# Gated cross-attention block: values by seven block products, the output projection in one place

## Chip, core and metric

The kernel runs on one NeuronCore of a Trainium2 chip. The metric is the device time of one execution in microseconds; the median of three runs is given. Profiles are one execution each.

The engines are called as in the profile: PE is TensorE (PEld its weight loads), DVE is VectorE, ACT is ScalarE, POOL is GpSimd, SP is SyncE, which only issues DMAs here.

## What is computed

There are 8 batches of a 512 x 2048 matrix x (features by sequence), a context c of the same shape, and a mask. All is float32.

```python
xn = layernorm(x)                              # over the sequence axis
q, k = Wq @ patch(xn) + bq, Wk @ patch(xn) + bk   # patches of 128 columns, 256 rows
v = Wv @ patch(c) + bv                         # 256 rows
attn = softmax(mask(q_h.T @ k_h / sqrt(32)))   # 8 heads of 32 rows, 128 x 128 in each patch
o = gelu(v_h @ attn.T)
x1 = x + tanh(g_xattn) * mask * (Wo @ o + bo)
flat = layernorm(x1)                           # over the sequence again; rows are the 512 features
s = softmax(flat @ router.T + rb)              # 64 experts
w = the 8 largest of s, the others zero
out = x1 + tanh(g_ffn) * (flat * sum(w) + w @ expert_bias)
```

## The kernel before

The sequence of each batch is cut into chunks of 512 columns, four per batch, 32 in all. A chunk has two halves of 256 columns (two patches each). One pass of the main loop, a *slot* `g`, handles the scores and the exponentials of one half: `ch = g // 2`, an even slot for the first half and an odd one for the second. Work of other chunks is mixed into the slot by hand. There is no automatic scheduler: each engine runs its instructions in the order of the program text, and tiles bring the waits.

In slot `g` of chunk `ch` the program does, in this order of the text:

1. `scores(g)`: four PSUM banks `sc0` to `sc3` (pool `ps_sc`, one buffer each) take the mask product (L433) and the score products (L442).
2. `weigh(g-2)` and `weighed(g-2)`: attention times values into a bank `tr`, copied to `o` by ACT (L515).
3. `maxima`, `exps` (DVE L454, ACT L463), `divide` (a reciprocal on DVE, L471, and a 128 x 1024 product on POOL, L472), and `turn`/`turned` (PE transposes of the slot before, L486, and ACT copies, L492).
4. `queries_and_keys(ch+1, h)`: half of the rows of q and k of the next chunk, by seven block products in place of eight. Its sums s1, s5, u2, u3 are on DVE, u4 on POOL (L387), and the second half of k (L395) adds u4. `sums_of_x` prepares the sums of xn on POOL (L300 to L305).
5. `values(ch+1, h)`: v of one half of the next chunk, 8 products of 128 x 256 (L410) into a bank `mm`, evicted by one DVE addition (`values_out`, L419).
6. `attend`: the output projection of the chunk before, 4 row blocks `m` of 512 columns (L534), each evicted by DVE (L540) into `t` and added to x on POOL (L543). Blocks 0 and 1 stand at the end of the odd slot; blocks 2 and 3 follow the scores of the next even slot.
7. `turn_x`, `logits`, `statistics2` (L553), and, per batch in turn, `aggregate` (L246 to L254), `gather`, `choose`, `select`, `turn_weights`: the router for the batch that is complete. `fin` is `g % 8` for that batch: 2 aggregates, 3 gathers, 4 selects.
8. `scale_x` (POOL, L678) and `mix` (PE L691, DVE L702, then the store): the expert mix of a batch that is twelve slots behind.

Reads of x for the statistics of the next batch (`stats_x`, L263) are on DVE near the slot's end. The last two slots, 62 and 63, are written out after the loop.

The pools that matter: `ps_mm` and `ps_tr` have two banks each, `ps_sc` four; `cx` (a half of c) has two buffers, `o` two, `mk` four. All large loads and stores are issued on SP.

Of the kernel before, what the change touches and what calls it, by code (L numbers as in the profile page):

```python
# [35 lines left out]
def flamingo_gated_kernel(  # L36
# [74 lines left out]

    def load_cx(ch, h, queue=nc.sync):
        t = work.tile([P, NM, HW], F32, tag="cx", name=f"cx_{ch}_{h}")
        s0 = (ch % NCH) * CW + h * HW
        queue.dma_start(t, rows_of(c, ch // NCH, slice(s0, s0 + HW)))
        cxs[ch, h] = t

    def load_mask(ch):
        t = work.tile([P, CW], F32, tag="mk", name=f"mk_{ch}", bufs=4)
        nc.sync.dma_start(t, masks[ch // NCH, :, columns(ch)].to_broadcast([P, CW]))  # L120
        mks[ch] = t
# [33 lines left out]
    load_first_x(0)  # L155
    load_cx(0, 1)
    nc.sync.dma_start(wq_sb, wqT.rearrange("(m p) e -> p m e", p=P))
    nc.scalar.dma_start(wk_sb, wkT.rearrange("(m p) e -> p m e", p=P))
    load_first_x(1)

    def load_rest():
        load_cx(1, 0)
        load_first_x(2)
        load_first_x(3)
        load_mask(0)
        nc.sync.dma_start(bv_sb, bv.partition_broadcast(P))
        with nc.allow_non_contiguous_dma(reason="short bias vectors onto partitions"):
            nc.sync.dma_start(bq_sb, bq.rearrange("(t p) -> p t", p=P))
            nc.sync.dma_start(bk_sb, bk.rearrange("(t p) -> p t", p=P))
            nc.sync.dma_start(bo_sb, bo.rearrange("(t p) -> p t", p=P))  # L170
        nc.sync.dma_start(gates[:, 0:1], g_xattn.partition_broadcast(P))
        nc.sync.dma_start(gates[:, 1:2], g_ffn.partition_broadcast(P))
        nc.sync.dma_start(rb_sb, rb.partition_broadcast(P))
        load_mask(1)
# [11 lines left out]
    for i in range(2):  # L186
        nc.vector.tensor_copy(
            ident2[i * E : (i + 1) * E, :], ident[i * E : (i + 1) * E, i * E : (i + 1) * E]
        )
    ones = const.tile([P, P], F32, name="ones")  # L190
    nc.vector.memset(ones, 1.0 / S)

# [228 lines left out]


    pairs = {}

# [86 lines left out]
    def weighed(g):  # L511
        ch, hf = g // NH, g % NH
        if hf == 0:
            os_[ch] = work.tile([P, NE, CW], F32, tag="o", name=f"o_{ch}")
        nc.scalar.copy(  # L515
# [78 lines left out]

    def gather(b, ms=range(NM)):

        t = experts[b]
        if 0 in ms:
            t["pg"] = ps_tr.tile([P, NM, E], F32, tag="tr", name=f"pg_{b}")
            t["lg"] = small.tile([P, NM, E], F32, tag="lg", name=f"lg_{b}", bufs=1)  # L600
        for m in ms:
            nc.tensor.matmul(  # L602
                t["pg"][:, m, :], lgT[b][:, m * P : (m + 1) * P], ident2, start=True, stop=True
            )

    def gathered(b):
        t = experts[b]
        nc.scalar.copy(t["lg"], t["pg"])
        t["pg"] = t["lg"]

# [44 lines left out]
    def turn_weights(b):  # L655
        t = experts[b]
        rest = t.pop("rest")
        wT = small.tile([P, NM // 2, P], F32, tag="wT", name=f"wT_{b}", bufs=1)
        pw = product([P, NM // 2, P], f"pw_{b}", None if late else 1)
        for mp in range(NM // 2):  # L660
# [115 lines left out]
    def centre_router():  # L776

        pr = ps_tr.tile([P, E], F32, tag="tr", name="pr")
        nc.tensor.matmul(pr, ones, rwsum, start=True, stop=True)
        nc.vector.tensor_tensor(  # L780
            rw_sb, rw_sb, pr[:, None, :].to_broadcast([P, NK, E]), ALU.subtract
        )
# [6 lines left out]
    for g in range(NG - NH):  # L789
# [14 lines left out]
        pch = ch - 1 if not even and ch >= 1 else None  # L804

        vals = [] if (nxt, h) == (1, 0) or nxt == last else [(nxt, h)]
        b4 = ch // NCH - 1
# [12 lines left out]
        if even:  # L820
            if nxt > 1:
                load_cx(nxt, 1)
            if nxt < last and nxt + 1 >= NCH:
                load_xn(nxt + 1)
        elif nxt < last:
            load_cx(nxt + 1, 0)
        if even and NCH <= ch - 1:
            load_xr(ch - 1)

# [17 lines left out]
        if even:  # L847
            if xch is not None:
                for m in (2, 3):
                    attend(xch, m)  # L850
                del os_[xch], mks[xch]
            exps(g, 1)
            exps(g, 2)
            if g > 0:
                mask(nxt)
            turn_(0)
            turn_(1)
# [4 lines left out]
            if g > 0:  # L862
                divide(g, 0)
            if g == 0:
                load_mask(2)
        else:
# [17 lines left out]
        def between(i):  # L884
            if even:
                if g == 0 and i == 0:
                    divide(g, 0)
                    mask(nxt)
                turn_x_(i)
            elif i == 0:  # L890
                if g == 1:
                    divide(g, 0)
                turn_(1)
                if fin == 3:
                    gather(b4)
                    gathered(b4)
                if pch is not None:
                    gelu(pch)
            else:
                turn_(2)  # L900
                if pch is not None and nxt < last:
                    load_mask(nxt + 1)

# [32 lines left out]
        if even:  # L936
            turn_x_(2)
            for c_, h_ in vals:
                values(c_, h_, 0, 0)
                turn_(2)  # L940
                values(c_, h_, 1)
            if not vals:
                turn_(2)
            if nxt < last and (nxt + 1) % NCH:
                norm(nxt + 1, (0, 1))
            for c_, h_ in vals:
                values_out(c_, h_)
            if fin == 4:
                stats()
            if fin == 4:  # L950
                turn_weights(b4)
            turn_x_(3)
            turn_(3)
            if nxt < last and (nxt + 1) % NCH:
                norm(nxt + 1, (2, 3))
            if fin == 4:
                for k in steps:
                    scale_x(mb, k)
        else:
# [3 lines left out]
            if fin == 3:  # L963
                choose_exps(b4)
            for c_, h_ in vals:
                values(c_, h_, 0, 0)
                values(c_, h_, 1)
                values_out(c_, h_)
            if pch is not None:
                for m in (0, 1):  # L970
                    attend(pch, m, r=m + 1)
            if nxt < last:
                sums_of_x(nxt + 1, 1)
                sums_of_x(nxt + 1, 2)
        if g == 1:
            nc.scalar.activation(wo_sb, wo_sb, AF.Copy, scale=tgates[:, 0:1])
        if g == 2:
            router_sums()
        if g == 3:
            centre_router()  # L980
# [21 lines left out]
    maxima(h0, (2, 3))  # L1002
    exps(h0, 0)
    exps(h0, 1)
    for m in (2, 3):
        attend(z - 2, m, tag=t_raw)
    divide(h0, 0)
    turn_(h0 - 1, 0, 1)
    exps(h0, 2)
    values(z, 0, 0)  # L1010
    turn_(h0 - 1, 2)
    exps(h0, 3)
    values(z, 0, 1)
    values_out(z, 0)
    turn_(h0 - 1, 3)
    divide(h0, 1)

# [6 lines left out]
    exps(g, 0)  # L1024
    mix(b - 1, 2)
    turn_(h0, 1)
    exps(g, 1)
    divide(g, 0)
    values(z, 1, 0)
    turn_x(z - 2, 0, nc.vector)  # L1030
    exps(g, 2)
    values(z, 1, 1)
    values_out(z, 1)
    exps(g, 3)
    divide(g, 1)
    turn_(h0, 2)
    turn_x(z - 2, 1, nc.vector)
    turn_(h0, 3)
    turn_x(z - 2, 2, nc.vector)
    gelu(z - 1)  # L1040
    mix(b - 1, 3)
    load_xr(z)
    turn_x(z - 2, 3, nc.vector)
    weigh(h0)
# [112 lines left out]
```

## Time and profile before

| what | us |
|---|---|
| median of 3 runs | 1337.61 |
| lowest to highest | 1336.63 to 1337.97 |
| the profiled execution, device time | 1337.72 |
| its span, first to last instruction | 1335.9 |
| PE busy | 1306.5 |
| DVE busy | 887.2 |
| ACT busy | 836.0 |
| POOL busy | 793.1 |
| an even slot in the middle (655.98 to 675.90) | 19.92 |

The mean granted TensorE clock is 0.995 of full speed. An idle time in the profile's rows stands in brackets, with what ended it. Busy times overlap: they say how much an engine has to do, not which one the others wait for. The order in which one engine's rows stand and the start times tell that.

### The profile page before, as it was taken

To read this page: it belongs to the slowest core of one execution; us is meant where nothing else is said; L and a number is where in the kernel's file an instruction comes from. 1 tells how busy PE (TensorE), PEld (TensorE's weight loads), DVE (VectorE), ACT (ScalarE), POOL (GpSimd) and SP (SyncE) were. 2 spreads that over 40 slices of the span, in tenths; PEclk is the share of its full clock that TensorE was granted. 3 is DMA by queue.
4 is the path that set the end of the run, shared out by engine and by line. 5 is a ranking of instruction groups with operands and counts; after the bars stand their busy time and mean duration, and the time that the engine had idled before them with its cause. 6 is when DMAs were issued, how large, how long until landed. Compare 5 with 4: busy or idle time off the path is not lost.

```text
span 1335.9 us, 26509 instructions
## 1 busy us (share of the span) xinstructions
PE 1306.5 (98%) x9802; PEld 953.6 (71%) x9802; DVE 887.2 (66%) x1815; ACT 836.0 (63%) x2843; POOL 793.1 (59%) x802
## 2 busy tenths in 40 slices
PE   7999999999999999999999999999999999999997
PEld 4677777777777777777777777777777777777653
DVE  5666666576766766677666676667676675666566
ACT  2567756666755666756667566667656767656653
POOL 3545556565566755667555667556566665566652
PEclk8999999999999999999999999999999999999999
DMA  9423332334443534443534443524544423332124
GB/s 290 117 73 124 98 103 99 131 105 133 150 163 115 166 102 136 150 146 131 166 100 138 151 148 130 166 89 135 165 146 132 156 65 120 135 112 87 64 80 173
DMA packets 109729, 173.32 MB, mean 130 GB/s; under 512 B 9248, under 2 KB 43680, under 8 KB 109472
## 3 DMA queue, kind: packets, MB, share of 16 engines
q1 hardware_dynamic: 107536, 168.75, 39.1%
q10 hardware_dynamic: 2064, 2.88, 0.6%
q8 instruction: 77, 1.26, 0.4%
q14 instruction: 52, 0.43, 0.1%
HBM read 138.06 MB, written 33.55 MB: 128 GB/s over the span
## 4 chain that ended last, share of the span: by engine, by line
PE 93%; DVE 3%; ACT 2%; DMA 1%; issue 0%; DVEq 0%; ACTq 0%
PE qk L373 27%; PE po L534 17%; PE pv L410 15%; PE pt L486 8%; PE pa L505 5%; PE pb L691 5%; PE pl L572 4%; PE sc L442 4%; PE px L558 4%; PE sc L433 2%; ACT at L463 1%; PE pf L339 1%; DMA cx<-in_ctx 1%; DVE st L553 1%; DVE st L263 1%; PE pg L602 1%
## 5 line engine op out<-in xcount | busy, mean ns | idle before, releaser
L472 POOL TENSOR_TENSOR at<-at,rsum 128x1024 f32<-128x1024 f32 x128 | 244.3, 1908 | 282.2 <-DVE rsum L471 259.6
L463 ACT ACTIVATE at<-sc,nmx 128x128 f32<-128x128 f32 x1024 | 364.9, 415 | 5.8 <-DVE nmx L454 5.8
L463 ACT ACTIVATION_READ_ACCUMULATOR at<-sc,nmx 128x1 f32 x1024 | 261.4, 255 | 0.0
L410 PE MATMUL pv<-wv_sb,cx 128*128 128x256 f32 x1024 | 242.7, 386 | 9.8 <-DMA cx<-in_ctx 9.6
L534 PE MATMUL po<-o,wo_sb 128*128 128x512 f32 x512 | 234.0, 599 | 0.0
L410 PEld LDWEIGHTS pv<-wv_sb,cx 128*128 128x128 f32 x1024 | 191.4, 194 | 33.8 <-DMA cx<-in_ctx 10.0
L543 POOL TENSOR_TENSOR xr<-t,xr 128x512 f32<-128x512 f32 x124 | 160.4, 1294 | 88.7 <-DVE t L540 88.2
L515 ACT COPY o<-pa 128x512 f32<-128x512 f32 x64 | 37.5, 585 | 258.2 <-PE pa L505 258.2
L492 ACT COPY atT<-pt 128x512 f32<-128x512 f32 x256 | 151.4, 622 | 56.2 <-PE pt L486 55.7
L454 DVE TENSOR_REDUCE nmx<-sc 128x4 f32<-128x512 f32 x256 | 158.7, 682 | 12.0 <-PE sc L442 12.0
L534 PEld LDWEIGHTS po<-o,wo_sb 128*128 128x128 f32 x512 | 94.2, 190 | 100.1 <-issue 92.8
L540 DVE SCALAR_TENSOR_TENSOR t<-po,bo_sb,mk 128x512 f32<-128x512 f32 x128 | 95.9, 750 | 100.6 <-PE po L534 99.9
L486 PEld LDWEIGHTS pt<-ident,at 128*128 128x128 f32 x1024 | 122.0, 141 | 56.9 <-issue 36.4
L486 PE MATMUL pt<-ident,at 128*128 128x128 f32 x1024 | 150.8, 275 | 1.3 <-ACT atT L492 1.1
L563 ACT COPY x1T<-px 128x512 f32<-128x512 f32 x120 | 70.3, 585 | 118.8 <-PE px L558 117.1
L373 PE MATMUL qk<-xt,wq_sb 128*128 128x256 f32 x496 | 128.2, 381 | 1.3 <-DVE u L381 1.3
L373 PE MATMUL qk<-xn,wk_sb 128*128 128x256 f32 x496 | 127.6, 380 | 0.0
L373 PE MATMUL qk<-xn,ws 128*128 128x256 f32 x496 | 127.3, 379 | 0.0
L373 PEld LDWEIGHTS qk<-xn,ws 128*128 128x128 f32 x496 | 94.2, 190 | 12.8
L702 DVE TENSOR_TENSOR xr<-pb,xr 128x512 f32<-128x512 f32 x124 | 79.2, 684 | 33.0 <-PE pb L691 33.0
L373 PEld LDWEIGHTS qk<-xn,wk_sb 128*128 128x128 f32 x496 | 89.3, 190 | 10.0 <-DVE lgT L588 0.3
L678 POOL TENSOR_SCALAR xr<-xr,xa,xd 128x512 f32<-128x512 f32 x120 | 94.4, 797 | 0.8
(119 smaller groups left out, 2008.4 us busy)
## 6 DMA issues: line engine op xcount, KB each, us to landing
cx<-in_ctx SPq DMA_DIRECT2D x63, 512.0 KB, 5.4
out_dram<-xr SPq DMA_DIRECT2D x60, 512.0 KB, 3.5
raw<-in_x SPq DMA_DIRECT2D x112, 256.0 KB, 3.5
xn<-in_x SPq DMA_DIRECT2D x28, 1024.0 KB, 7.5
xr<-in_x SPq DMA_DIRECT2D x28, 1024.0 KB, 7.8
mk<-in_mask_Bx1x_ff SPq DMA_DIRECT2D x32, 256.0 KB, 5.4
xr<-in_x SPq DMA_DIRECT2D x10, 256.0 KB, 5.9
out_dram<-xr SPq DMA_DIRECT2D x7, 256.0 KB, 2.3
```

What stands on the lines that cost most here:

```text
L373: nc.tensor.matmul(out_, w_[:, j, es], xb[:, j, :], start=(j == 0), stop=(j == NM // 2 - 1))
L410: nc.tensor.matmul(pv[:, i, :], cx[:, m, i * W : (i + 1) * W], wv_sb[:, m, :], start=(m == 0), stop=(m == NM - 1),)
L454: nc.vector.tensor_reduce(p["nmx"][:, r, :, :], p["sc"][r], AX.X, ALU.max, negate=True)
L463: nc.scalar.activation(p["at"][i][:, h, :], p["sc"][r][:, i, e, :], AF.Exp, bias=p["nmx"][:, r, i, e : e + 1], accum_out=p["rsum"][:, i, h ...
L472: (engine or nc.gpsimd).tensor_tensor(p["at"][i], p["at"][i], rs[:, :, None].to_broadcast([P, H, W]), ALU.mult)
L486: nc.tensor.transpose(pt[:, r, :], p["at"][i][:, e * HR + r, :], ident)
L492: nc.scalar.copy(p["atT"][i][:, e * HR : (e + 1) * HR, :], p.pop("pt"))
L534: nc.tensor.matmul(po[:, cs], wo_sb[:, e, m * P : (m + 1) * P], os_[ch][:, e, cs], start=(e == 0), stop=(e == NE - 1),)
L540: nc.vector.scalar_tensor_tensor(t[:, cs], po[:, cs], bo_sb[:, m : m + 1], mks[ch][:, cs], ALU.add, ALU.mult)
L543: (engine or nc.gpsimd).tensor_tensor(xc, t[:, cs], xc, ALU.add)
L678: nc.gpsimd.tensor_scalar(xc, xc, a, d, ALU.mult, ALU.add)
L702: nc.vector.tensor_tensor(xc, pt, xc, ALU.add)
```

## The change

- `values` and `values_out` give way to `values_by_seven` for chunks 2 to 31. It computes both halves of the chunk `ch` itself, in its even slot, by seven products of blocks in four banks `sc0` to `sc3` (in chunk 31 in banks `mm`). A block is 256 columns of c by 256 rows of features times 256 features by 128 outputs, in matmuls of 128 columns. The sums of the weights are made once (`sums_of_wv`, slot 2), the sums of c per chunk on POOL in the odd slot before (`sums_of_c`), and one more sum of c on POOL between the products.
- Both halves of c are loaded at the start of the odd slot before their chunk.
- All four blocks of `attend` stand at the end of the odd slot, in the banks `sc0` to `sc3`, ahead of `mix`.
- The mask of the next chunk is formed after the third pair of q and k products; `mk` has three buffers and is loaded at the even slot's start. The fillers `turn` and `turn_x` move to new places.
- The router's gathered logits are read from PSUM by `choose`; the ACT copy `gathered` is gone.
- The third half of c, `cx_1_0`, is loaded early into the buffer of `o`, which now has one buffer.
- In the last two slots the parts stand in a new order.

```diff
-    def load_cx(ch, h, queue=nc.sync):
-        t = work.tile([P, NM, HW], F32, tag="cx", name=f"cx_{ch}_{h}")
+    def load_cx(ch, h, queue=nc.sync, tag="cx"):
+        t = work.tile([P, NM, HW], F32, tag=tag, name=f"cx_{ch}_{h}", bufs=1 if tag == "o" else 2)
...
+    load_cx(1, 0, tag="o")
     nc.sync.dma_start(wq_sb, wqT.rearrange("(m p) e -> p m e", p=P))
...
     def load_rest():
-        load_cx(1, 0)
...
+    def sums_of_wv():
+        nc.gpsimd.tensor_tensor(wt3, v22, v12, ALU.subtract)
+        nc.gpsimd.tensor_tensor(v12, v12, v11, ALU.subtract)
+        nc.gpsimd.tensor_tensor(wt2, v22, v12, ALU.subtract)
+        nc.gpsimd.tensor_tensor(wt4, v21, wt2, ALU.subtract)
+
+        nc.vector.tensor_tensor(bv_sb[:, e2], bv_sb[:, e2], bv_sb[:, e1], ALU.subtract)
...
+    def sums_of_c(ch):
...
+        nc.gpsimd.tensor_tensor(t1, a21, a22, ALU.add)
+        nc.gpsimd.tensor_tensor(t2, t1, a11, ALU.subtract)
+        nc.gpsimd.tensor_tensor(a21, a11, a21, ALU.subtract)
+
+    def values_by_seven(ch, between, banks=range(4)):
...
+        def pair(*ops):
+            pv = product([P, len(ops), NPP, P], f"pv_{ch}_{len(banks)}", banks.pop(0))
+            for n, (a, w_) in enumerate(ops):
+                for i in range(NPP):
+                    for j in range(NM // 2):
+                        nc.tensor.matmul(
+                            pv[:, n, i, :], a[:, j, i * W : (i + 1) * W], w_[:, j, :],
+                            start=(j == 0), stop=(j == NM // 2 - 1),
+                        )
+            return [pv[:, n, :, :] for n in range(len(ops))]
+
+        bias = [bv_sb[:, None, e].to_broadcast([P, NPP, P]) for e in (e1, e2)]
+        p1, p6 = pair((c0[:, d1, :], v11), (t2, wt2))
+        nc.vector.tensor_tensor(s1, p1, bias[0], ALU.add)
+        nc.vector.tensor_tensor(u2, p6, s1, ALU.add)
+
+        nc.gpsimd.tensor_tensor(t2, c0[:, d2, :], t2, ALU.subtract)
+        between(0)
+        p2, p5 = pair((c0[:, d2, :], v21), (t1, v12))
+        nc.vector.tensor_tensor(vt[0][:, :, e1], p2, s1, ALU.add)
+        nc.vector.tensor_tensor(s5, p5, bias[1], ALU.add)
+        nc.gpsimd.tensor_tensor(u4, u2, s5, ALU.add)
+        between(1)
+        p7, p4 = pair((c1_[:, d1, :], wt3), (c1_[:, d2, :], wt4))
+        u3 = work.tile([P, NPP, P], F32, tag="s1", name=f"vu3_{ch}", bufs=1)
+        nc.vector.tensor_tensor(u3, p7, u2, ALU.add)
+        nc.gpsimd.tensor_tensor(vt[1][:, :, e2], u3, s5, ALU.add)
+        nc.vector.tensor_tensor(vt[1][:, :, e1], p4, u3, ALU.add)
+        between(2)
+        (p3,) = pair((t2, v22))
+        nc.vector.tensor_tensor(vt[0][:, :, e2], p3, u4, ALU.add)
...
         if even:
             if nxt > 1:
-                load_cx(nxt, 1)
+                load_mask(nxt)
...
-        elif nxt < last:
-            load_cx(nxt + 1, 0)
...
+        elif nxt >= 2:
+            for i in range(NH):
+                load_cx(nxt, i)
...
         if even:
-            if xch is not None:
-                for m in (2, 3):
-                    attend(xch, m)
-                del os_[xch], mks[xch]
+            turn_(0)
             exps(g, 1)
             exps(g, 2)
-            if g > 0:
-                mask(nxt)
-            turn_(0)
             turn_(1)
...
         def between(i):
             if even:
-                if g == 0 and i == 0:
-                    divide(g, 0)
+                if i == 0:
+                    if g == 0:
+                        divide(g, 0)
+                    turn_(2)
+                else:
                     mask(nxt)
-                turn_x_(i)
+                    turn_x_(0)
...
+            turn_x_(1)
+
+            def between_values(i):
+                if i == 0:
+                    turn_x_(2)
+                    if nxt < last and (nxt + 1) % NCH:
+                        norm(nxt + 1, (0, 1))
+                elif i == 1:
+                    turn_(3)
+                    if fin == 4:
+                        stats()
+                        turn_weights(b4)
+                else:
+                    turn_x_(3)
+                    if nxt < last and (nxt + 1) % NCH:
+                        norm(nxt + 1, (2, 3))
+
+            if vch is not None:
+                values_by_seven(vch, between_values)
...
-            for c_, h_ in vals:
-                values(c_, h_, 0, 0)
-                values(c_, h_, 1)
-                values_out(c_, h_)
-            if pch is not None:
-                for m in (0, 1):
-                    attend(pch, m, r=m + 1)
...
             if nxt < last:
                 sums_of_x(nxt + 1, 1)
                 sums_of_x(nxt + 1, 2)
+            if nxt >= 2:
+                sums_of_c(nxt)
+            if pch is not None:
+                for m in range(NM):
+                    attend(pch, m, r=m)
+                del os_[pch], mks[pch]
```

## The prediction

> **What bounds the kernel now.** I read the page first, then the TensorE groups by shape, then the timeline of one engine at a time over one steady even slot (it starts at 655.98 us), then the places where TensorE stood still.
>
> ```profile
> PE 1306.5 (98%) x9802; PEld 953.6 (71%) x9802; DVE 887.2 (66%) x1815; ACT 836.0 (63%) x2843; POOL 793.1 (59%) x802
> ```
>
> ```profile
> L410 PE MATMUL pv<-wv_sb,cx 128*128 128x256 f32 x1024 | 242.7, 386 | 9.8 <-DMA cx<-in_ctx 9.6 <-DVE xr L702 0.3
> ...
> L602 PE MATMUL pg<-ident,lgT 128*128 128x64 f32 x64 | 8.1, 270 | 0.2 <-DVE lgT L590 0.2
> ```
>
> TensorE works 98% of the span, so the issue of matmuls sets the time. In the slot its queue is one unbroken row:
>
> ```profile
> 655.98 0.40 PE L433 MATMUL sc<-mneg,negw 32*128 32x512 bf16 x4
> ...
> 658.20 3.70 PE L534 MATMUL po<-o,wo_sb 128*128 128x512 f32 x8
> ...
> 669.98 1.89 PE L410 MATMUL pv<-wv_sb,cx 128*128 128x256 f32 x8
> ...
> 672.14 1.89 PE L410 MATMUL pv<-wv_sb,cx 128*128 128x256 f32 x8
> ...
> 675.90 0.39 PE L433 MATMUL sc<-mneg,negw 32*128 32x512 bf16 x4
> ```
>
> The reader sees a slot of 19.92 us, in it 3.5 us of output projection (658.20 to the transposes at 661.74) and 3.45 us of values; the odd slot takes 19.99. POOL and VectorE look free, but each runs its own queue in order, and the change loads those queues. Below, +t is time since the slot's start. First POOL, the odd slot's end and the even slot:
>
> ```profile
> 648.98 1.90 POOL L472 TENSOR_TENSOR at<-at,rsum 128x1024 f32<-128x1024 f32 x1 [1.28 <-DVE rsum L471]
> ...
> 664.14 1.69 POOL L678 TENSOR_SCALAR xr<-xr,xa,xd 128x512 f32<-128x512 f32 x2
> 665.80 1.89 POOL L472 TENSOR_TENSOR at<-at,rsum 128x1024 f32<-128x1024 f32 x1
> 667.65 0.72 POOL L387 TENSOR_TENSOR u<-u,s 128x256 f32<-128x256 f32 x1
> ...
> 671.02 1.90 POOL L472 TENSOR_TENSOR at<-at,rsum 128x1024 f32<-128x1024 f32 x1 [1.28 <-DVE rsum L471]
> ```
>
> Then VectorE in that slot: the k that needs POOL's u4, the reciprocal, the statistics, and last the value eviction.
>
> ```profile
> 663.06 1.38 DVE L314 TENSOR_SCALAR mneg<-m 128x512 bf16<-128x512 f32 x1
> ...
> 668.84 0.47 DVE L395 SCALAR_TENSOR_TENSOR ks<-qk,bk_sb,u 128x256 f32<-128x256 f32 x1
> ...
> 670.68 0.20 DVE L471 RECIPROCAL rsum<-rsum 128x8 f32<-128x8 f32 x1
> 670.79 2.42 DVE L553 BATCH_NORM_STATS2 st<-xr 128x6 f32<-128x512 f32 x4
> ...
> 674.32 0.67 DVE L419 TENSOR_TENSOR vT<-pv,bv_sb 128x512 f32<-128x512 f32 x1
> ```
>
> u4 is ready at +12.4 and k takes it at +12.9 after u3: in time. That u4 is late after the change is my main step.
>
> **TensorE's share.** Removed per chunk: 32 instructions of 256 columns. Eight start to start take 1.73 us (669.98 to 671.70), 0.216 each: 6.9 us. Added: 7 products x 2 panels x 2 rows of blocks x 2 instructions = 56 of 128 columns. None such is in the trace with full rows and a real product; bounds are the transposes (128 columns, 0.109 start to start) and pg (64 columns, the same 128-wide weight load, eight in 1.10 us, 0.11 start to start). I take 0.111: 6.2 us, 0.7 saved, 20 us over 30 chunks. [...]
> The projection only moves: four po of 1.72 us in the odd slot replace values of 3.45 and two po, same sum. It starts at +12.0 there, where gelu ends at +11.9 (646.80 and 1.06): about 0.1 us waiting per odd slot. In the even slot the second transposed pair now follows pa at once and its bank waits for ACT's copy of pa; the trace shows that once (eight transposes take 1.43 instead of 1.04 at 65.89): +0.4. TensorE's even slot alone: scores, pa 2.2; transposes to 3.5; qk and their fillers to 10.85; pairs at 10.85, 13.06, 15.28; last product at 17.49; mix 18.4 to 19.45. So 0.47 less than before.
>
> **POOL.** Per chunk, 3 sums of c and one more of t2 at 1.24 us (the pitch of the 128x512 rows), u4 and one vT at 0.73: +6.5 us, 195 over the kernel. Busy share would be about 74%; the order is what costs. In the odd slot it stands: second divide (starts 7.0 us before the even slot, as 648.98), four xt, three sums of c, four xr (all four t are there by +0). So: divide to -5.1; xt to -0.2; sums to +3.5; xr to +8.4; scale (1.55) to +9.95; first divide (1.87) to +11.8; u4 to +12.55. u4 comes as before, but TensorE now brings u4's consumer its product at +9.1 instead of +12.2, for the projection has left. VectorE stands at k from +8.9 to +12.6.
>
> **VectorE.** Added 7 evictions of 256 columns (0.42 each by L381's pitch) less 2 of 0.69: +1.6 us a chunk. Behind k, by the pitches of the shown rows: k 12.65; the masks, now placed behind k, 13.3 (POOL still in qs) to 14.1 (0.43 each: mneg took 0.43 at 25.93 with POOL quiet, 1.38 under a POOL sum; with 1.38 all is 0.95 later); q and k x mask to 15.05; reciprocal 15.16; statistics to 17.5; raw to 18.7. Only then the value evictions, one per 0.43: s1, u2, vT, s5, u3, vT done by 21.3; the last needs product p3. POOL's second divide waits for that reciprocal: 15.25 to 17.1, t2 to 18.35; TensorE's p3 runs 18.45 to 19.35 (0.95 of waiting), mix to 20.4. Last eviction ends at 21.75. The next scores take the four banks of the values, so they stop at the fourth until 21.85. **The even slot becomes 21.85: +1.9.** What lay behind the old stall-free row was 3.5 us of projection covering u4; it is gone.
>
> Two even slots in every eight differ. In the third of a batch (695.9) the router's statistics are aggregated on POOL, ahead of t2 in its queue, and they wait for VectorE:
>
> ```profile
> 714.93 0.23 POOL L248 TENSOR_SCALAR v<-mv 128x4 f32<-128x4 f32 x1 [2.10 <-DVE mv L246]
> ...
> 717.59 1.52 POOL L678 TENSOR_SCALAR xr<-xr,xa,xd 128x512 f32<-128x512 f32 x2
> ```
>
> The seven small steps take 2.66 us. mv comes at 19.2, so t2 ends at 23.2, p3 at 24.2, last eviction 24.75, slot 24.85: **+4.9**, with TensorE still for 5.8 us. What such a stop costs besides:
>
> ```profile
> 1236.55 0.44 PE L661 MATMUL pw<-ident,rest 128*128 128x128 f32 x2 [2.95 <-DVE rest L648]
> ```
>
> ```profile
> 1237.00:1241.00 4.00, 4.00 (x31) 2.08 (x31) 0.76 (x2) 1.65 (x3) 3.44 (x6) 0.57 0.00 0
> ```
>
> After 2.95 us of idling the granted clock was 0.57 in the next 4 us. [...]
> In the fifth slot (selection) no scale stands before u4 and no statistics before the evictions: about 20.75 against 20.14, +0.6; at the last one (21.08 before, TensorE waited 2.95) -0.3.
>
> **The start.** The third piece of c waited for a free buffer (issued 12.97, landed 19.44; TensorE idled 3.09, and ran the next 16 matmuls in 6.78 instead of 3.6). With its own buffer TensorE can go on at 16.4 and is then bound by the fourth xn (done 30.75): pf ends near 34.3 instead of 39.9. The extra 512 KB ahead of x delays x on a full DMA by up to 1.8; I take -5 (bounds -6, 0). Slot 2 loses its values: -2 (TensorE 3.45; POOL's four weight sums there take 2.9). End, g 61 to 63: -0.7.
> **At nothing:** 7 copies of pg (0.37, ACT idles behind; choose then reads PSUM, as four of 0.28 at the end already do, and its bank is wanted again 5 us later by the fourth po); both c loads in one place on SP (land 5.4 us after issue, by +9.5, wanted at +19.8 of the odd slot; raw loads behind them keep most of a slot); the mask load at +1.8, landed by +9, wanted at +13; if it came late, all moves with it.
>
> **Sum.** 12 plain x 1.9 = 22.8; aggregation 6 x 4.9 + 4.2 = 33.6, clock 14; selection 6 x 0.6 - 0.3 = 3.3; chunks 2 to 4, with no scale or mix, 1 each = 3; odd slots 3; start, slot 2, end -7.7. +72 on the profiled 1337.7 (span 1335.9 and 1.8 around; median 1337.6): 1410.
>
> **Rivals.**
> Late u4 as worked out (0.79): 1385 to 1432.
> TensorE still the bound (0.09): if u4 came by +10.2, the last eviction would end before mix, and every even slot be 19.45: -13.6 + 3 - 7.7, 1319. For it: POOL is only 59% busy. Against it: its queue order above needs 17.6 us from the divide's end to u4.
> Only the aggregation stalls (0.10): VectorE catches up in plain slots, 7 x 4.2 - 7.7: 1359. The values not shorter (0.111 wrong) would be covered in all but the TensorE case.
> Stalls and savings equal: 0.02. 0.2% is about what a measurement here can tell from none.
> Range 1362 to 1432.
>
> **What would show it.** Right: in the even slot VectorE's k waits 3 to 4 us for POOL u; the scores wait for VectorE's last vT; p3 waits for POOL's t2; clock drops after aggregation slots; POOL near 990 us. Wrong: no idle time at the scores, even slots below 20 us, or pv instructions of 128 columns above 0.12 apart.

## The result, and the profile after

The changed kernel takes 1438.91 us (median of 4 runs, 1437.4 to 1441.92) beside 1337.12 for the kernel before on the same chip (1336.59 to 1337.97): a ratio of 1.0765, 95% interval 1.0752 to 1.0778. It is 101.8 us slower. I had forecast 1410 with a range of 1362 to 1432: the direction and the main chain of waits were right, the size was 29 us short. The forecast failed at the transpose pw in the selection slots and at the kernel's edges, above all in slot 3; both are told below. The profiled execution took 1441.92 us and has a span of 1440.1, 104.2 more than before.

From the page: busy times, the chain that ended last, and one group (busy us, mean ns, then the idle time just before it and what ended it).

```profile
PE 1333.8 (93%) x10522; PEld 980.8 (68%) x10522; DVE 897.3 (62%) x1966; ACT 831.6 (58%) x2836; POOL 975.1 (68%) x986
...
POOL 38%; PE 37%; DVE 17%; issue 5%; ACT 2%; DMA 1%; POOLq 0%; SPq 0%; DVEq 0%; ACTq 0%
...
L468 PE MATMUL pv<-wv_sb,cs 128*128 128x128 f32 x480 | 73.0, 300 | 45.9 <-POOL cs L479 45.9
```

TensorE fell from 98% to 93% of the span, yet no other engine is full: POOL, the first in the chain, is busy 68% of the time. The order in its queue holds TensorE. The last line is one of the places: 45.9 us ahead of p3, the last of the seven products, for t2, the sum of c that POOL makes at L479. In a plain even slot (neither aggregation nor selection; its first mask matmul is at 485.16), POOL's timeline:

```profile
489.20 4.95 POOL L619 TENSOR_TENSOR xr<-t,xr 128x512 f32<-128x512 f32 x4
494.13 1.54 POOL L749 TENSOR_SCALAR xr<-xr,xa,xd 128x512 f32<-128x512 f32 x2
495.62 1.92 POOL L546 TENSOR_TENSOR at<-at,rsum 128x1024 f32<-128x1024 f32 x1
497.47 0.74 POOL L386 TENSOR_TENSOR u<-u,s 128x256 f32<-128x256 f32 x1
...
500.83 1.90 POOL L546 TENSOR_TENSOR at<-at,rsum 128x1024 f32<-128x1024 f32 x1 [1.93 <-PE pt L560]
502.69 1.27 POOL L479 TENSOR_TENSOR cs<-cx,cs 128x512 f32<-128x512 f32 x1
```

VectorE's, in the same slot:

```profile
498.25 0.48 DVE L394 SCALAR_TENSOR_TENSOR ks<-qk,bk_sb,u 128x256 f32<-128x256 f32 x1 [3.20 <-POOL u L386]
...
500.61 2.42 DVE L629 BATCH_NORM_STATS2 st<-xr 128x6 f32<-128x512 f32 x4
502.95 1.27 DVE L262 BATCH_NORM_STATS2 st<-raw 128x6 f32<-128x512 f32 x2
504.13 0.41 DVE L476 TENSOR_TENSOR vs<-pv,bv_sb 128x256 f32<-128x256 f32 x1
...
506.56 0.42 DVE L493 TENSOR_TENSOR vT<-pv,vu 128x256 f32<-128x256 f32 x1
```

And TensorE's:

```profile
496.10 1.06 PE L468 MATMUL pv<-wv_sb,cx 128*128 128x128 f32 x8
497.00 1.06 PE L468 MATMUL pv<-wt,cs 128*128 128x128 f32 x8
...
504.01 1.16 PE L468 MATMUL pv<-wv_sb,cs 128*128 128x128 f32 x8 [1.07 <-POOL cs L479]
...
507.04 0.37 PE L507 MATMUL sc<-mneg,negw 32*128 32x512 bf16 x1 [0.15 <-DVE vT L493]
```

Read the three together: u4 (497.47), the sum that k needs, comes behind POOL's four sums of x, the scaling and the first divide; k waits 3.20 us for it; all evictions of the values stand behind k and the statistics; p3 waits for t2, and the next scores for the last eviction. Twice in each eight slots it is worse. In the aggregation slot TensorE stands 5.43 us and then runs its next matmuls at half clock; in the selection slot it waits ahead of pw, the transpose of the chosen weights.

```profile
417.30 2.08 PE L468 MATMUL pv<-wv_sb,cs 128*128 128x128 f32 x8 [5.43 <-POOL cs L479]
...
460.58 0.41 PE L732 MATMUL pw<-ident,rest 128*128 128x128 f32 x2 [2.42 <-DVE vu L477]
```

Busy time by stretch, right after the 5.43 us (the stretch and its length, busy time and instructions of PE, PEld, DVE, ACT and POOL, then the granted clock, here 0.52, the DMA share and GB/s):

```profile
417.30:421.30 4.00, 4.00 (x16) 2.33 (x20) 0.42 (x1) 0.00 (x0) 2.83 (x4) 0.52 0.00 0
```

I measured all slots from the fourth mask matmul of one `scores` to that of the next. "g%8 = 2" are the aggregation slots, "g%8 = 4" the selection slots, from g = 10 on.

| part | forecast, us more than before | measured |
|---|---|---|
| 12 plain even slots | 22.8 | 19.1 (21.0 to 21.9 where g%8 = 6, 20.6 to 21.5 where g%8 = 0, before 19.92) |
| 7 aggregation slots, with the clock | 47.6 | 47.1 (24.5 to 27.2 each) |
| 7 selection slots | 3.3 | 23.9 (22.96 to 24.75 each, before 20.14) |
| chunks 2 to 4, odd slots | 6 | 6.3 |
| start, slots 1 to 3, end | -7.7 | +7.8 |
| sum | 72 | 104.2 |

Three parts are near the forecast. The two others, 20.6 and 15.5 us off, hold more than the whole miss of 32.

### The profile page after: what moved, and what is told of

Same layout as the page of the kernel before. It is cut to its first block, busy times and chain, and to the rows that moved or that the text cites. A ratio compares the mean times of both kernels' runs of the same rounds, so it can differ in the third digit from the quotient of the medians.

```text
span 1440.1 us, 28337 instructions
## 1 busy us (share of the span) xinstructions
PE 1333.8 (93%) x10522; PEld 980.8 (68%) x10522; DVE 897.3 (62%) x1966; ACT 831.6 (58%) x2836; POOL 975.1 (68%) x986
## 4 chain that ended last, share of the span: by engine, by line
POOL 38%; PE 37%; DVE 17%; issue 5%; ACT 2%; DMA 1%; POOLq 0%; SPq 0%; DVEq 0%; ACTq 0%
PE qk L372 14%; POOL xr L619 10%; POOL at L546 8%; PE pl L648 4%; PE pt L560 4%; DVE st L629 3%; PE pv L468 3%; PE pa L579 3%; POOL cs L446 2%; POOL xt L304 2%; POOL xt L301 2%; POOL xt L299 2%; POOL cs L445 2%; POOL cx L447 2%; PE sc L516 2%
## 5 line engine op out<-in xcount | busy, mean ns | idle before, releaser
L537 ACT ACTIVATION_READ_ACCUMULATOR at<-sc,nmx 128x1 f32 x1024 | 265.3, 259 | 0.0
L610 PE MATMUL po<-o,wo_sb 128*128 128x512 f32 x512 | 228.0, 597 | 0.0
L566 ACT COPY atT<-pt 128x512 f32<-128x512 f32 x256 | 159.4, 630 | 28.4 <-PE pt L560 28.4
L560 PE MATMUL pt<-ident,at 128*128 128x128 f32 x1024 | 159.7, 279 | 7.8 <-ACT o L591 5.0
L528 DVE TENSOR_REDUCE nmx<-sc 128x4 f32<-128x512 f32 x256 | 158.8, 682 | 13.1 <-PE sc L516 12.6
L619 POOL TENSOR_TENSOR xr<-t,xr 128x512 f32<-128x512 f32 x124 | 153.8, 1274 | 8.2 <-DVE t L616 8.2
L468 PE MATMUL pv<-wv_sb,cs 128*128 128x128 f32 x480 | 73.0, 300 | 45.9 <-POOL cs L479 45.9
L372 PEld LDWEIGHTS qk<-xn,ws 128*128 128x128 f32 x496 | 94.8, 191 | 13.1
L468 PEld LDWEIGHTS pv<-wv_sb,cs 128*128 128x128 f32 x480 | 65.4, 212 | 50.4 <-POOL cs L479 50.4
L372 PEld LDWEIGHTS qk<-xt,wq_sb 128*128 128x128 f32 x496 | 86.1, 193 | 14.3 <-DVE u L380 7.3
```

The costliest lines, as they stand in the source:

```text
L372: nc.tensor.matmul(out_, w_[:, j, es], xb[:, j, :], start=(j == 0), stop=(j == NM // 2 - 1))
L468: nc.tensor.matmul(pv[:, n, i, :], a[:, j, i * W : (i + 1) * W], w_[:, j, :], start=(j == 0), stop=(j == NM // 2 - 1),)
L528: nc.vector.tensor_reduce(p["nmx"][:, r, :, :], p["sc"][r], AX.X, ALU.max, negate=True)
L537: nc.scalar.activation(p["at"][i][:, h, :], p["sc"][r][:, i, e, :], AF.Exp, bias=p["nmx"][:, r, i, e : e + 1], accum_out=p["rsum"][:, i, h ...
L560: nc.tensor.transpose(pt[:, r, :], p["at"][i][:, e * HR + r, :], ident)
L566: nc.scalar.copy(p["atT"][i][:, e * HR : (e + 1) * HR, :], p.pop("pt"))
```

## The experiments

The base is the changed kernel (median 1438.9, its profiled execution 1441.9) unless another is named. The kernel before took 1336.2 to 1337.5 us beside all of them. e1 to e6 are one profiled execution each, and the changed kernel's own four differ by up to 4.5 us; where a difference is of that size, I go by the slots in the traces. e7 to e12 are medians of four or five executions.

**e5: one more sum on POOL ahead of u4.** Is POOL's queue the bound? It does a sum twice, with the same result.

```diff
         nc.gpsimd.tensor_tensor(t1, a21, a22, ALU.add)
+        nc.gpsimd.tensor_tensor(t1, a21, a22, ALU.add)
```

> The changed kernel with the first of the three sums of c done twice on POOL, per chunk one 128x512 addition of 1.24 us more, ahead of the xr additions and u4; nothing else. Theory (every us that u4 is later makes the even slot a us longer): +1.24 in each of 30 even slots, 36 us more, near 1475. Rival (u4 is beside the path, VectorE's amount of work sets the slot): no change, 1439.

Measured 1483.35: 44.4 us more, or about 1.5 us in each of 30 chunks. The plain slots went from 21.87 to 23.22 and from 21.45 to 22.80, 1.35 each. One instruction of 1.24 us on an engine that is idle a third of the time is paid in full.

**e4: the seven products undone alone.** Values by eight products of 256 columns in `sc0` and `sc1`, no sums of c; the rest of the change stays.

```diff
-                values_by_seven(vch, between_values)
+                values_by_eight(vch, between_values)
...
-            if nxt >= 2:
-                sums_of_c(nxt)
```

> Undoes the seven products alone: each chunk's values are the plain products of 256 columns in the even slot, in banks sc0 and sc1, with one eviction per half; no sums of c, no t2, no sums of the weights. The projection and all else stay as in the changed kernel. Theory: without the three sums of c in POOL's queue u4 is ready 3.7 us earlier, at +8.9, in time; even slots are set by TensorE at about 20.2, no long stop at aggregation; near 1351. Rival (moving the projection out of the even slot is itself the loss): stays above 1410.

Measured 1362.28: 76.6 of the 101.8 us go with the seven products and their sums. 25 stay, more than the 14 I expected, in three places: even slots of 20.33 instead of 19.92, selection slots of 21.08 instead of 20.14, and slot 3, still 26.4.

**e1: u4 ahead of the scaling and the first divide.**

```diff
-            if fin != 4:
-                for k in steps:
-                    scale_x(mb, k)
             if g > 0:
-                divide(g, 0)
+                divide(g, 0, parts="r")
...
         queries_and_keys(nxt, h, between)
+        if even and g > 0:
+            divide(g, 0, parts="m")
+        if even and fin != 4:
+            for k in steps:
+                scale_x(mb, k)
```

> In even slots POOL's first divide (128x1024) and the two scale_x stand behind u4 and qs instead of ahead of them; same work on every engine. Theory (POOL's queue makes u4 late, VectorE stops at k, everything behind it is late): u4 comes 3.4 us earlier, plain even slots fall from 21.9 and 21.5 to about 19.7, aggregation slots from 27.1 to 22 to 24, selection slots from 23 to 21; about 67 us less, near 1372. Rival (VectorE's added evictions are simply too much work for the slot): no change, 1439. Rival (the 128-column products are the cost): no change, 1439.

Measured 1424.59, a miss. u4 was in time and k no longer waited, but the plain slots came down only to 20.65 and the aggregation slots to 26.4. VectorE's timeline of e1, then POOL's, show what was late next:

```profile
490.85 0.47 DVE L394 SCALAR_TENSOR_TENSOR ks<-qk,bk_sb,u 128x256 f32<-128x256 f32 x1
...
492.06 2.00 DVE L313 TENSOR_SCALAR mneg<-m 128x512 bf16<-128x512 f32 x1
```

```profile
491.70 2.08 POOL L549 TENSOR_TENSOR at<-at,rsum 128x1024 f32<-128x1024 f32 x1
```

The mask step now coincides with POOL's long product and takes 2.00 us instead of 0.43 (499.22 in the changed kernel). My prediction had 1.38 for this case as a bound and did not follow it up.

**e6: e1 with the mask formed earlier**, behind the eviction of s5, and loaded at the odd slot's end.

```diff
                 if i == 0:
...
+                    mask(nxt)
                     turn_(2)
                 else:
-                    mask(nxt)
                     turn_x_(0)
```

> As e1 (u4 ahead of the divide and the scales), and the mask pair on VectorE stands behind s5 instead of behind k; the mask is loaded at the odd slot's end. Theory (in e1 u4 was in time, but the mask's second step then waited 1.6 us for POOL's divide to end, where before POOL stood idle): the masks fall in VectorE's idle time, plain even slots go from 20.65 to about 19.6, near 1400 with the aggregation stops still in. Rival (the seven evictions behind the statistics are what is left): stays at 1424.

Measured 1396.41. The total is near the 1400 expected, but by luck: the plain slots are 20.45 and 20.03 where I had 19.6, and give only 3.8 of the 28 us gained over e1. The rest comes from slots that I had not counted: aggregation (26.4 to between 24 and 25.5), selection, slots 4 to 8, and slot 3 (28.05 to 24.48). What holds is that u4 was one of two things in series, and the mask the other.

**e2: the aggregation behind the products of the values.**

```diff
-        if fin == 2:
-            nmean, rs = aggregate(st2.pop(b4), NCH, f"2_{b4}")
-            experts[b4] = {"nmean": nmean, "rs": rs}
...
             if vch is not None:
                 values_by_seven(vch, between_values)
...
+            if fin == 2:
+                nmean, rs = aggregate(st2.pop(b4), NCH, f"2_{b4}")
+                experts[b4] = {"nmean": nmean, "rs": rs}
```

> The router's aggregation stands behind the value products in VectorE's and POOL's queues, in 7 slots. Theory (t2 waits behind the aggregation in POOL's queue, TensorE stops 5.4 us at p3 and then runs at half clock): those 7 slots fall from 27.1 to about 21.9, 36 us less, near 1403. Rival (the stop is the late VectorE queue, the aggregation only adds to it): only the half clock goes, 2.3 us each, near 1423.

Measured 1403.58, 35.3 less, as expected. The aggregation slots became plain ones (27.1 to 21.44), 38.3 us less in the seven, and the half clock behind them went (mean granted clock 0.988; 0.972 in the changed kernel). Seven small steps on POOL had cost that, because they take 2.7 us (413.34 to 416.02), wait 2.10 us for VectorE before that, and t2 is queued behind them. The selection slots became 4.8 us longer in sum: behind the same stop ahead of pw (17.0 us in the seven, in both traces) the clock was now halved in six of seven slots, in place of three.

**e3: the transposed weights of the choice (pw) in a bank `mm`** instead of `sc0`.

```diff
-        pw = product([P, NM // 2, P], f"pw_{b}", None if late else 0)
+        pw = product([P, NM // 2, P], f"pw_{b}", None)
```

> The router's transposed weights go to a bank of the pool mm instead of bank sc0, which still holds the first value products. Theory (in selection slots TensorE stops at this transpose until VectorE has emptied sc0, 0.9 us after its own input is ready, long enough in three of seven slots to halve the clock): selection slots 23.0 and 24.6 fall to about 22.1, 11 us less, near 1428. Rival (it waits for its input, rest): no change, 1439.

Measured 1431.18, 7.7 us under the median and 10.7 under the profiled execution. The seven selection slots are 10.9 us shorter, as expected: 22.1 each (the first 22.3), and the 24.6 to 24.75 with half clock are gone. pw still waits 1.55 us in each, for `rest`, its input.

**e7: e6, e2 and e3 together**, and pa of the even slots in a bank `mm`. Does TensorE alone bound the kernel then?

> e6, with the aggregation behind the products (e2), the router's transposed weights in a bank of mm (e3), and pa of even slots in a bank of mm, so that the second transposed pair no longer waits 0.4 us for ACT's copy. Theory: TensorE alone sets every even slot, 19.1 to 19.2 in plain and aggregation slots, 20.3 in selection slots; odd slots 20.06; the edges cost 9 as in the changed kernel; near 1335, level with the kernel before. Rival (another engine's queue takes over): even slots above 19.8, above 1350.

Measured 1353.96, ratio 1.0131 (1.0113 to 1.0149). The single gains (42.5, 35.3, 7.7) add up to 85.5 and this one is 84.9, but that is no proof of separate stops: e7 also moves pa, and by the spans of the traces the single gains are 94.7 and this one 88.2. They overlap somewhat, for e6 and e2 both shorten the aggregation slots. And e7 is 19 us above the expectation and still slower than before. TensorE's timeline of e7, then POOL's:

```profile
474.44 1.16 PE L468 MATMUL pv<-wv_sb,cs 128*128 128x128 f32 x8 [0.53 <-POOL cs L479]
```

```profile
469.78 1.52 POOL L752 TENSOR_SCALAR xr<-xr,xa,xd 128x512 f32<-128x512 f32 x2
471.26 1.89 POOL L549 TENSOR_TENSOR at<-at,rsum 128x1024 f32<-128x1024 f32 x1
473.12 1.27 POOL L479 TENSOR_TENSOR cs<-cx,cs 128x512 f32<-128x512 f32 x1
```

t2 stands behind the scaling and a divide that nothing needs before the next slot.

**e8: e7 with the router's sums of slot 2 behind that slot's maxima.** It tests one reason for the long slot 3.

> e7, with the sum over the router's weights (1.94 us on VectorE) moved in slot 2 from the slot's end to behind the maxima. Theory (slot 3 is 26.5 instead of 19.1 because VectorE enters it late, TensorE idles 4.9 us there and runs at half clock): slot 3 falls by 3 to 6, near 1330. Rival (slot 3 waits for something else): as e7.

Measured 1354.13, the same as e7; slot 3 stayed at 24.5. The theory fell: VectorE then waited 2.27 us for a load of `raw` at the same place, ahead of the maxima.

**e9: e7 with POOL's order by what is wanted first**: t2 behind the first divide, then the scaling and the value sums, the second divide last; the third sum of c behind u4; pw between the last products.

```diff
+        if vch is not None:
+            third_sum_of_c(vch)
         if even and g > 0:
             divide(g, 0, parts="m")
-        if even and fin != 4:
-            for k in steps:
-                scale_x(mb, k)
...
-        divide(g, 1)
+        divide(g, 1, parts="r" if even and fin != 4 else "rm")
...
                 if i == 0:
+                    if fin != 4:
+                        for k in steps:
+                            scale_x(mb, k)
...
+            if fin != 4:
+                divide(g, 1, parts="m")
```

> Against e7: in the even slot GpSimd now does u4, qs, the third sum of c, the first divide, t2, the scaling of x, the fourth and fifth sums of the value products, and only then the second divide; the weights of the choice are turned between the third pair of products and the last. Theory (GpSimd's order is what the even slots of e7 still wait for; TensorE is 0.7 us shorter in them): t2 is there before p3, the stops of 0.53 us ahead of p3, 0.47 ahead of the x transposes and 0.58 ahead of pw go, even slots of 19.3 to 19.6 instead of 20.03 to 20.45, selection slots about 20.2 instead of 21.35, and with the edges as in e7 about 1328 us, below the kernel before (1336.5). Rival (the queue merely passes the delay on: VectorE's mask and its k times m now stand beside another GpSimd instruction, or the odd slot's divides come later): even slots still 20.0 to 20.4 and about 1350 us.

Measured 1346.71, ratio 1.0074 (1.006 to 1.0088); between the two. (One of its five executions took 3191.04 us, with no cause on record; the other four lie between 1345.25 and 1347.13.) The plain slots are 19.66, under the 19.92 of before for the first time. The selection slots stayed at 21.43: there t2 still stood behind a divide and the choice. And VectorE still did this ahead of the fifth qk product; the rows are from the selection slot at 412.91, and the plain slots lost time by it too (19.66 us here, 19.32 in e11):

```profile
419.23 0.20 DVE L549 RECIPROCAL rsum<-rsum 128x8 f32<-128x8 f32 x1 [2.52 <-ACT at L540]
419.35 0.38 DVE L379 COPY s<-qk 128x256 f32<-128x256 f32 x1
419.77 0.42 DVE L380 TENSOR_TENSOR u<-qk,s 128x256 f32<-128x256 f32 x1
```

The evictions of q and k stand behind a reciprocal that waits for ScalarE's exponentials. In the kernel before, half of the projection stood ahead of these products.

**e10: e9 with eight products.** What are seven worth when nothing waits for them?

> e9 with the values by eight products of 256 columns, and without the sums of c and of Wv: the rest of the change in the good order. It measures what the seven products are worth where nothing waits for them. Theory (TensorE alone bounds the slot in both): 0.7 us more than e9 in each of 29 even slots, so about 20 us above e9, some 1348 us. Rival (the even slot is bounded by VectorE or GpSimd, not by TensorE): within 5 us of e9, or below it.

Measured 1356.08, 9.4 us above e9. In the plain slots the forecast holds: 20.33 against 19.66, 0.67 us; both have the same short stop at the fifth qk product there, so the difference is TensorE's work. The selection slots go the other way (20.52 against e9's 21.43), which is why the whole is only half of the expected 20.

**e11: the last two stops of e9 removed.** The reciprocal stands behind the mask; in the selection slots the choice stands behind t2 and the divide last. In slot 3 the first divide stands behind the evictions of k.

```diff
-            if g > 0:
-                divide(g, 0, parts="r")
...
                     mask(nxt)
+                    if g > 0:
+                        divide(g, 0, parts="r")
                     turn_(2)
...
-        if fin == 4:
-            select(b4)
...
+                    if fin == 4:
+                        select(b4)
+                    else:
                         for k in steps:
                             scale_x(mb, k)
```

> e9 with three things moved back on VectorE and GpSimd: in the even slots the first reciprocal of the divides stands behind the mask (so behind the evictions of q and k, L379 and L380, which waited there for ScalarE's exponentials), in slot 3 behind the evictions of k; in the selection slots the choice's steps stand behind t2 and its second divide behind the scaling of x. Theory (in e9 the plain even slots lose 0.43 us ahead of the fifth product of q and k, and the selection slots 1.32 us ahead of p3, and TensorE is bound by nothing else): plain even slots 19.2 to 19.3 instead of 19.66, selection slots about 19.6 instead of 21.43, slot 3 about 23 instead of 24.3, and 1346.7 less 23 times 0.43, 8 times 1.8 and 1, about 1321 us, about 1 per cent below the kernel before. Rival (the moved reciprocal delays GpSimd's first divide and t2 again, or the choice's steps come too late for pw): plain slots 19.6 and selection slots above 20.5, 1338 to 1346 us.

Measured 1326.37, ratio 0.9923 (0.991 to 0.9937): faster than the kernel before, by 0.8%. The plain slots are 19.32, as expected. The selection slots are 20.02 where I had 19.6, and slot 3 did not move (24.48 where I had 23), so the whole is 5 us above the expectation.

**e12: e11 with four steps of VectorE taken from ahead of slot 3's maxima.**

```diff
+        if g == 3:
+            read_x(n_carried)
+            router_sums()
+            difference_of_bias()
+            write_ones()
         if vch is not None:
             third_sum_of_c(vch)
...
-            router_sums()
             sums_of_wv()
...
-        read_x(len(pieces))
+        if g == 2:
+            carried.extend(pieces)
+        else:
+            read_x(len(pieces))
```

> e11 with four steps of VectorE taken out of the way of slot 3's maxima: the second piece of statistics of the next batch, the router's sums, the difference of the bias and the tile of ones stand behind slot 3's products of q and k instead of ahead of its scores' maxima (ones instead of behind the last po). Theory (slot 3 is bounded by VectorE's queue: maxima at 75.69 us in e11 where the scores are there by 70.8, then ScalarE's exponentials and gelu): TensorE's stops of 2.34 and 1.14 us and the 1.08 us at pr go, with the half clock after them; slot 3 about 20.5 instead of 24.48, the kernel about 1322 us. Rival (something else ends last there, ScalarE's own queue or the load of the pieces of x): slot 3 above 23 and 1325 us or more.

Measured 1323.27, ratio 0.9899 (0.9883 to 0.9916), the fastest of all, 1.0% below the kernel before. Slot 3 came down by 2.2 us to 22.25, a little over half of what was expected: the stop at the qk product is gone, but TensorE now waits for ScalarE's gelu, and the projection behind it runs in part at half clock: its sixteen matmuls take 8.83 us, where sixteen take 7.12 at 676.03, a loss of 1.7 us, or 3.4 us at half clock. TensorE's timeline of e12:

```profile
81.45 8.83 PE L617 MATMUL po<-o,wo_sb 128*128 128x512 f32 x16 [1.71 <-ACT o L611]
```

From its page, with POOL busier than in the changed kernel and TensorE at 98% again:

```profile
PE 1293.5 (98%) x10522; PEld 960.4 (73%) x10522; DVE 938.3 (71%) x1966; ACT 830.8 (63%) x2836; POOL 993.5 (75%) x986
```

## Where the prediction was right, and which steps failed

**Right: u4 late on POOL, and all behind it.** In the plain slot k was forecast at +12.65 and came at +13.1; t2 to end at 18.35 and p3 to start at 18.45, p3 came at +18.85; the last eviction to end at 21.75, it ended at +21.8. The slot is 21.87 against 21.85 (21.45 in the slots where g%8 = 0, which had the same forecast). e5 shows that POOL's queue carries it, e1 and e6 that u4 and the mask are the links.

**Right: the aggregation slots.** t2 was forecast to end at 23.2 and ended at +23.2; TensorE stood 5.43 us where I had 5.8. For the clock the sum has 14 us, 2 us a slot, an estimate that no run shows by itself; what the trace shows is a granted clock of 0.50 for 6.8 us in each of the seven, part of it waiting. e2 takes 38.3 us out of these slots, the stop and the clock together.

**Right: 128-column products cost 0.111 us.** Eight go in 0.89 us (496.10 to 497.00), and 0.67 us a slot is saved (e9 against e10; forecast 0.7). The matmuls of these eight start 0.111 to 0.112 us apart, each with a weight load of 128 full rows.

**Wrong: the selection slots, 3.3 forecast, 23.9 measured.** The step that failed is pw: the forecast put no wait ahead of it. TensorE stood there 2.42 us in each of the seven slots, 17 us in sum, and in three of them the clock halved behind it (granted 0.50 for 3.4 us from 284.6, 636.2 and 1161.8). Two things hold pw.

First, its input. `rest`, the end of the choice on VectorE, is done at +17.5 in the changed kernel, no later than before. But the change moved pw forward in TensorE's queue, from +17.9 to about +16.0, ahead of the third pair of products. VectorE's and TensorE's timelines of the kernel before, for the selection slot that starts at 736.70:

```profile
753.77 0.42 DVE L648 TENSOR_TENSOR rest<-lg,rest 128x256 f32<-128x256 f32 x1
```

```profile
754.59 0.38 PE L661 MATMUL pw<-ident,rest 128*128 128x128 f32 x2
```

VectorE's of the changed kernel, for the one that starts at 442.13 (its pw, at 460.58, is shown above):

```profile
459.21 0.42 DVE L719 TENSOR_TENSOR rest<-lg,rest 128x256 f32<-128x256 f32 x1
```

For `rest` to come earlier, u4 would have had to, since the choice stands behind k. The forecast counted on that: without the scaling, u4 was to end at +11.0 by its terms (12.55 less 1.55). But I let POOL's second divide start as in a plain slot. In the odd slot before a selection, `choose` stands ahead of that divide's reciprocal on VectorE, so POOL waits, and its chain runs later. POOL's timeline of the same slot:

```profile
436.37 1.90 POOL L546 TENSOR_TENSOR at<-at,rsum 128x1024 f32<-128x1024 f32 x1 [3.40 <-DVE rsum L545]
...
453.84 0.73 POOL L386 TENSOR_TENSOR u<-u,s 128x256 f32<-128x256 f32 x1
```

The divide starts 5.8 us before the slot, not 7.0, and u4 ends at +12.4: what the missing scaling gives back is taken by the late start.

Second, its bank. The change puts pw in bank `sc0` where p1 and p6 lie, and VectorE evicts u2 from there only behind k and the choice: 0.87 us more (2.42 less the 1.55 that stay in e3).

e3 sizes the bank at 10.9 us, its half clock included. The 1.55 us for `rest` that stay in each slot make up 10.8 of the 13.0 us that e3's selection slots still have over the kernel before. In e9, where pw stands behind the third pair, TensorE waits for neither. The late divide was not run alone.

**Wrong: the edges, -7.7 forecast, +7.8 measured.** The step that failed: I counted TensorE instructions removed and took them as time, where TensorE was not the bound.
- Slot 2 did lose its values, 3.8 us. Slot 3 took 7.4 back. In the changed kernel (TensorE, then VectorE):

```profile
84.33 2.07 PE L372 MATMUL qk<-xt,wq_sb 128*128 128x256 f32 x4 [4.93 <-DVE u L380]
...
98.81 0.41 PE L852 MATMUL pr<-rwsum,ones 128*128 128x64 f32 x2 [1.07 <-DVE ones L850]
```

```profile
75.59 1.94 DVE L845 TENSOR_REDUCE rwsum<-rw_sb 128x64 f32<-128x1024 f32 x1
77.44 0.76 DVE L434 TENSOR_TENSOR bv_sb<-bv_sb 128x128 f32<-128x128 f32 x1
78.33 1.34 DVE L262 BATCH_NORM_STATS2 st<-raw 128x6 f32<-128x512 f32 x2
79.59 2.46 DVE L528 TENSOR_REDUCE nmx<-sc 128x4 f32<-128x512 f32 x4
```

  The scores are there by 73.9, their maxima start at 79.59 behind three other steps, and the exponentials, the reciprocal and the eviction u follow. 6.8 us of half clock (granted 0.50 from 83.2 to 90.1) come on top. The tile of ones, which the change writes behind the last eviction in slot 3, costs 1.07, and I had costed it at nothing without naming it. Of the 7.4 us, about 2 are back in e6 (24.48 there), and 4.3 in e12. Slot 1 is 1.2 us longer too, but not in e6 to e12.
- The start was forecast at -5. It is -2.8 in this execution: TensorE waited 1.88 us for the second part of xn (at 24.96) and ran on at half clock (granted 0.50 from 25.2 to 28.6). In the traces of all twelve experiments, whose start is nearly the same, it is -4.1 to -5.0 (in e12 the first scores stand at 35.8 against 40.8 before). So the term was about right, and the changed kernel's own trace is the exception.
- The end was forecast at -0.7 for slots 61 to 63. Slots 61 and 62 are 3.1 and 2.8 us longer, for they took work over from the tail; the tail lost that work (some 5 us of matmuls) and is just as long, 67.7 us: there TensorE waits for other engines, and runs 6.8 us at half clock (granted 0.50) from 1380.3 on. TensorE's timeline of the changed kernel:

```profile
1380.11 0.98 PE L634 MATMUL px<-ident,xr 128*128 128x128 f32 x4 [1.49 <-DVE x1T L637]
1382.59 1.11 PE L560 MATMUL pt<-ident,at 128*128 128x128 f32 x4 [1.50 <-ACT atT L566]
```

**The rivals.** "TensorE still the bound" at 1319 describes what the change is worth once the order of POOL and VectorE fits it: e11 and e12, which also move two banks, stand at 1326 and 1323. As written, the change is not that case. "Only the aggregation stalls" fell with the plain slots at 21.9.

Still open: the rest of slot 3 (22.25 in e12 against 19.14 before), the tail, and how much of the selection slots the late divide alone makes up.

## What to carry to other kernels

When work is moved to an engine that looks half idle, lay its queue out in time against the moment at which each result is wanted; what counts is what stands ahead of the one wanted result. Here nearly the same instructions made the kernel 7.6% slower or 1.0% faster, by order and by two banks (those of pw and pa). When a long block of matmuls leaves a place, ask for each step that it had covered who now waits for it, in every kind of slot, the rare ones too. And count removed instructions as time only where their engine is the one that ends last; at a kernel's start and end it often is not.

## What the runs showed of the hardware

- The mask step on VectorE has no data in common with POOL's instructions, and took longer in rows where POOL was in a long one. It took 0.43 us with POOL idle (at 67.81 in the kernel before; at 25.93, which I had read as quiet, POOL ran steps of 128x1), 0.83 and 1.37 in e7 (at 465.44 and 423.74) and 2.00 in e1 (at 492.06). In these last three it ended 0.28 to 0.29 us after POOL's instruction (in e1 at 494.06, POOL's at 493.78). The product of k and mask took 0.68 in the changed kernel with POOL idle (at 499.90) and 2.32 in e7 under a POOL product (at 426.46). So the bound of 1.38 from one row was too low.
- Half clock (granted 0.50) followed stops of TensorE of these lengths. In the changed kernel: 6.8 us of it with the five longest stops, 5.43 to 5.46 us (from 414.3 to 421.2 with the first), and with those of 4.93, 4.25 and 4.08 us (ahead of 84.33, 1290.38 and 240.85); 3.4 us of it after 1.88 us at the start and after three of the seven stops of 2.42 us ahead of pw. After the other four (at 460.58, 811.5, 986.1 and 1334.0) the clock stayed at 1.00. In the tail 6.8 us of it begin at 1380.29, with stops of 1.49 and 1.50 us ahead of 1380.11 and 1382.59. In the kernel before: 6.8 us with a stop of 3.09 (ahead of 19.48), 3.4 us after one of 2.95 (ahead of 1236.55). In slot 3 of e11, after 2.34 us, four qk matmuls took 2.08 us (at 79.00) where the four of the same shape at 77.91 in e12, without a stop, took 1.03.
- In the traces of the kernel before and of the changed kernel the stretches of half clock begin whole multiples of 3.41 us apart (414.32 and 588.40 in the changed kernel: 174.08, or 51 times 3.41). Why the same stop ahead of pw halved the clock in three slots and not in the four others, no run shows.
